# Attention weights as a product of two exponentials, with the transposed adjacency as the stationary operand

## Chip, core and metric

The kernel runs on one core of a Trainium2 chip. The metric is the device time of one execution in microseconds; the runs below are five executions of the kernel before the change. A profile is one execution recorded by the hardware profiler.

## What is computed

Four graph layers follow one another on 128 graphs of 64 nodes with 256 features. Each adds its result to its input and normalizes the rows. Layer 0 is five steps of a gated recurrent cell, layer 1 an MLP with RMS norm behind a neighbour sum, layer 2 a hyperbolic map, layer 3 an attention. The change is in layer 3:

```python
h = einsum('bnd,ed->bne', hidden, W_w) + W_b
a1, a2 = a_w[:Dh], a_w[Dh:]
e = h @ a1
f = h @ a2
logits = e[:, :, None] + f[:, None, :] + a_b[0]
u = mask * exp(logits)            # mask: the adjacency, 64 x 64 per graph
a = u / sum(u, axis=2, keepdims=True)
h_prime = einsum('bnm,bmd->bnd', a, h)
x = layernorm(x + h_prime)
```

## The kernel before

Two graphs share the 128 partitions as one block; four blocks make a group, so a group is 8 graphs, and 16 groups (NG) run through all four layers. The two graphs of a block lie on the diagonal quadrants of a 128 x 128 adjacency tile `edge` (`ed` in the code), zero elsewhere. `adjT` is its transpose, made once per group on TensorE (L620) and copied out of PSUM by VectorE (L623); L626 then turns `ed` into 0 and 1 for layer 0.

The functions `pe`, `turn`, `dve`, `act` and `pool` do not issue anything: they record an operation with its engine and an estimated cost in `Flow`. Every group is a stream of such operations, and the set-up is a stream of its own. `Flow.issue` then plans all streams together: `Plan.advance` picks, for an assumed clock of each engine, the operation that can start soonest, `ways` ranks operations by how much must follow them, several plans are kept side by side in stretches of 25 us, and the best one is issued. Up to four streams are open at once, and eight PSUM banks are shared among them (`bank`). So the order of instructions on each engine is that of the plan, and each engine works through its own in order. A change of any operation or cost lets the whole order be planned anew. Buffers come in slots by tag and group number modulo 3 (`unit`).

In layer 0 each of the five steps works on two halves of the group. `ps_hr` turns the state into rows, `ps_agg` sums neighbours with `ed`, `p_r`, `p_u`, `p_v`, `p_w`, `p_in` and `p_hn` are the gate products (L580), VectorE adds and ScalarE takes tanh. All matmuls are in fp32; the profile shows two records for each. Layer 1 has `ps_hid` and `ps_o` (line 300 is the helper `matmul`), layer 2 `ps_sup`. `layer_norm` takes statistics on VectorE, the power on GpSimd (L595, `rstd`), and writes half of the blocks on VectorE (L609), half on ScalarE (L605).

Layer 3, lines 890 to 927, for each group:

- L550 and L553: x3 is transposed on TensorE (`ps_T`), ScalarE copies it to `x3T`.
- For each of four blocks, `ps_a` (2 matmuls of 259 columns) gives h in 256 columns, one zero column, and the two sums e and f; VectorE adds the biases `wb_r` (L899) into `ho`. The added bias makes the zero column a column of ones.
- `ps_e` (L903): four transposes of one column of `ho`, repeated 128 times, bring the one sum to the free dimension; VectorE adds the other (L908) into `lg`, ScalarE takes the exponential (L911), VectorE multiplies by `adjT` (L915) into the quadrants of `ed`.
- `ps_att`: one matmul of 257 columns per block with `ed` as the stationary operand; column 256 is the sum of weights. VectorE takes the reciprocal (L922) and adds x3 (L923) to give y, and `layer_norm` follows.

The set-up loads weights and vectors (small vectors on GpSimd's DMA queue, L392 to L496), turns and combines the gate weights on TensorE, and works out the two extra columns of `wattT` and `wb_r` on VectorE (L525).

Of the kernel before, what the change touches and what calls it, by code (L numbers as in the profile page):

```python
# [13 lines left out]
AF = mybir.ActivationFunctionType  # L14
OP = mybir.AluOpType

P = 128
# [210 lines left out]
def kernel(  # L228
# [31 lines left out]
    nc = tc.nc  # L260
    B, N, D = x.shape
# [3 lines left out]
    NB = 4  # L265
    G = 2 * NB
    R = NB * P
    KD = D // P
# [11 lines left out]
    flow = Flow()  # L280
    quads = [slice(t * N, (t + 1) * N) for t in range(2)]


    def fixed(shape, name):
        return Buf(lambda: const.tile(shape, F32, name=name))

    def bank(name):
        return Buf(lambda: psum.tile([P, 512], F32, tag="bank", name=name), bank=True)

    def bufs(tag):  # L290
        return 2 if tag == "h" else 1

    def unit(tag, s, name, shape=(P, R), bufs=1):

        t = f"{tag}{s}"
        return Buf(lambda: work.tile(list(shape), F32, tag=t, name=name, bufs=bufs), slot=(t, bufs))


    def matmul(o, lhsT, rhs, k, nk):
        nc.tensor.matmul(o, lhsT, rhs, start=(k == 0), stop=(k == nk - 1))  # L300

    def pe(n, run, w, r):
        flow.op("PE", {512: 0.86, 256: 0.435, 257: 0.44, 128: 0.23}.get(n, 0.3), run, w, r)

    def turn(run, w, r):
        flow.op("PE", 0.11, run, w, r)

    def dve(n, run, w, r):
        flow.op("DVE", 0.16 + 0.00105 * n, run, w, r)

    def act(n, run, w, r):
        flow.op("ACT", 0.27 + 0.00077 * n, run, w, r)

    def pool(us, run, w, r=()):
        flow.op("POOL", us, run, w, r)
# [11 lines left out]
    def tiles_of(t):  # L327
        return t.rearrange("p (b n) -> p b n", n=P)

    def over(t, n):  # L330
        return t.unsqueeze(1).to_broadcast([P, n, t.shape[-1]])
# [19 lines left out]
    ident = Buf(lambda: ident_t)  # L351
# [26 lines left out]
    a12, na22, w_hn = gate_w("a12"), gate_w("na22"), gate_w("w_hn")  # L378
    a11, s1, s2, s3, s4, w_in = ([gate_w(f"{n}_{l}") for l in range(L)] for n in ("a11", "s1", "s2", "s3", "s4", "w_in"))

    wattT = fixed([P, KD, D + 3], "wattT")

    NV = 3 * KD
    NC = 2 * NV + 2 * KH
# [15 lines left out]
    for src, eng, tags in ((w_hh, "SP", ("h", "h")), (w_ih, "ACT", ("A", "B")), (att_w, "ACT", ("adjT",))):  # L400
        nf = src.shape[0] // P
        q = {"SP": nc.sync, "ACT": nc.scalar}[eng]
        for i, tag in enumerate(tags):
            n = min(4, nf - 4 * i)
# [53 lines left out]
    for l in range(L):  # L458
        ps = bank("ps_wmT")
# [9 lines left out]
        for k in range(KD):  # L469
            for i, n in ((0, 2 * D), (1, D)):  # L470
                ps = bank("ps_wmih")
# [19 lines left out]
    turned(att_w, KD, lambda i, k, ps: dve(256, lambda: nc.vector.tensor_copy(wattT[:, k, :D], ps[:, :D]),  # L491
                                           [(wattT, k)], [ps]))

    def everywhere(v, n, name, more=0):
        t = fixed([P, n + more], name)
        flow.op("POOL", 0.8, lambda: nc.gpsimd.dma_start(  # L496
            t[:, :n], bass.AP(tensor=v.tensor, offset=v.offset, ap=[[0, P], [1, n]])), [t])
        return t

    eps_c = everywhere(epsilon, 1, "eps_c")  # L500
    b2_r = everywhere(b2, D, "b2_r")
    wb_r = everywhere(att_b, D, "wb_r", 3)
    a_r = everywhere(a_w, 2 * D, "a_r")
    ab_c = everywhere(a_b, 1, "ab_c")

# [9 lines left out]
    junk_d = fixed([P, D], "junk_d")  # L515
# [1 line left out]

    pool(0.11, lambda: nc.gpsimd.memset(wattT[:, :, D:D + 1], 0.0), [(wattT, D)])  # L520
    pool(0.11, lambda: nc.gpsimd.memset(wb_r[:, D:D + 1], 1.0), [wb_r])
    for i in range(2):
        for o, k in ((wattT[:, 0, :], 0), (wattT[:, 1, :], 1), (wb_r.tile(), None)):
            src = wb_r if k is None else (wattT, k)
            dve(256, lambda o=o, i=i: nc.vector.scalar_tensor_tensor(  # L525
                junk_d.tile(), o[:, :D], 1.0, a_r[:, i * D:(i + 1) * D], OP.mult, OP.mult,
                accum_out=o[:, D + 1 + i:D + 2 + i]), [src if k is None else (wattT, (k, i))], [src, a_r])

    def group(g):
        s = g % NF  # L530

        def tiny(name, shape=(P, NB), dt=F32):
            t = f"{name}{s}"
            return Buf(lambda: small.tile(list(shape), dt, tag=t, name=f"{name}_{g}"), slot=(t, 2))

        def u(tag, name, shape=(P, R)):
            return unit(tag, s, f"{name}_{g}", shape, bufs(tag))

        def rows(tag, name):
            return u(tag, name, (P, NB, D))  # L540
# [4 lines left out]
        def feats_of(dst, src, n):  # L545

            ps = bank("ps_T")
            for j in range(2):
                for c in range(KD):
                    turn(lambda j=j, c=c: nc.tensor.transpose(  # L550
                        ps[:, c * HR + j * P:c * HR + (j + 1) * P], src[:, 2 * n + j, c * P:(c + 1) * P], ident.tile()),
                        [ps], [(src, 2 * n + j)])
            act(512, lambda: nc.scalar.copy(dst[:, :, half(n)], blocks_of(ps.tile())), [(dst, n)], [ps])  # L553

        def rows_of(src, n):

            ps = bank("ps_hr")
            for j in range(2):
                for c in range(KD):
                    turn(lambda j=j, c=c: nc.tensor.transpose(  # L560
                        ps[:, j * D + c * P:j * D + (c + 1) * P],
                        src[:, c, (2 * n + j) * P:(2 * n + j + 1) * P], ident.tile()), [ps], [(src, n)])
            return ps

        def aggregate(dst, src, b0, n):

            ps = bank("ps_agg")
            for j in range(2):
                for c in range(KD):
                    pe(128, lambda j=j, c=c: matmul(  # L570
                        ps[:, c * HR + j * P:c * HR + (j + 1) * P], src[:, b0 + j, c * P:(c + 1) * P],
                        ed[:, 2 * n + j, :], 0, 1), [ps], [(src, b0 + j), ed])
            act(512, lambda: nc.scalar.copy(dst[:, :, half(n)], blocks_of(ps.tile())), [(dst, n)], [ps])  # L573
            return ps
# [42 lines left out]
        ed = edge[s]  # L617
        ps = bank("ps_adjT")
# [3 lines left out]
        adjT = u("adjT", "adjT", (P, NB, P))  # L622
        dve(512, lambda ps=ps: nc.vector.tensor_copy(adjT.tile(), tiles_of(ps.tile())), [adjT], [ps])  # L623
        for t in range(2):
            q = quads[t]
# [123 lines left out]
        for n in range(2):  # L749
            ps = rows_of(hT, n)  # L750
            for j in range(2):
                b = 2 * n + j
# [5 lines left out]
        for t in range(2):  # L758
            q = quads[t]
# [3 lines left out]
        x1 = layer_norm(y0, "A", "n0")  # L763
# [8 lines left out]
        for i, tag in enumerate(("h", "h", "B", "A")):  # L772
            t = u(tag, f"hid{i}", (P, KD, R))
            hid += [(t, 0), (t, 1)]
        sqs = u("U", "sqs")
        for c in range(KH):
            ps = bank("ps_hid")
# [11 lines left out]
        ps = bank("ps_ss")  # L789
# [21 lines left out]
        for h in range(NB // 2):  # L811
            ps = bank("ps_o1")
            for j in range(2):
                b = 2 * h + j
# [4 lines left out]
            for j in range(2):  # L819
                b = 2 * h + j  # L820
# [36 lines left out]
        for h in range(NB // 2):  # L857
            for j in range(2):
                b = 2 * h + j
                pe(256, lambda b=b, j=j, ps=sup[h]: matmul(  # L860
                    ps[:, j * D:(j + 1) * D], adjT[:, b, :], tan[:, b, :], 0, 1), [sup[h]], [adjT, (tan, b)])
            for j in range(2):
                b = 2 * h + j
# [23 lines left out]
        x3 = layer_norm(y2, "B", "n2")  # L887


        x3T = u("agg", "x3T", (P, KD, R))  # L890
        for n in range(2):
            feats_of(x3T, x3, n)
        ho = u("h", "ho", (P, NB, D + 3))
        for b in range(NB):
            ps = bank("ps_a")
            for k in range(KD):
                pe(256, lambda ps=ps, b=b, k=k: matmul(
                    ps[:, :D + 3], x3T[:, k, b * P:(b + 1) * P], wattT[:, k, :], k, KD), [ps], [(x3T, b // 2), wattT])
            dve(256, lambda ps=ps, b=b: nc.vector.tensor_add(ho[:, b, :], ps[:, :D + 3], wb_r.tile()),  # L899
                [(ho, b)], [ps, wb_r])  # L900
        ps_e = bank("ps_e")
        for b in range(NB):
            turn(lambda b=b: nc.tensor.transpose(  # L903
                ps_e[:, b * P:(b + 1) * P], ho[:, b, D + 1:D + 2].to_broadcast([P, P]), ident.tile()), [ps_e], [(ho, b)])
        lg = u("U", "lg", (P, NB, N))
        for t in range(2):
            q = quads[t]
            dve(256, lambda q=q: nc.vector.tensor_tensor(  # L908
                lg[q], tiles_of(ps_e.tile())[q, :, q], ho[q, :, D + 2].unsqueeze(2).to_broadcast([N, NB, N]), OP.add),
                [(lg, t)], [ps_e, ho])  # L910
        act(256, lambda: nc.scalar.activation(lg.tile(), lg.tile(), AF.Exp, bias=ab_c.tile()), [lg], [lg, ab_c])  # L911

        for t in range(2):
            q = quads[t]
            dve(256, lambda q=q: nc.vector.tensor_mul(ed[q, :, q], lg[q], adjT[q, :, q]), [(ed, t)], [lg, adjT])  # L915
        y3 = rows("y", "y3")
        rd = tiny("rd")
        for b in range(NB):
            ps = bank("ps_att")
            pe(257, lambda ps=ps, b=b: matmul(ps[:, :D + 1], ed[:, b, :], ho[:, b, :D + 1], 0, 1),  # L920
               [ps], [ed, (ho, b)])
            dve(4, lambda ps=ps, b=b: nc.vector.reciprocal(rd[:, b:b + 1], ps[:, D:D + 1]), [(rd, b)], [ps])  # L922
            dve(256, lambda ps=ps, b=b: nc.vector.scalar_tensor_tensor(  # L923
                y3[:, b, :], ps[:, :D], rd[:, b:b + 1], x3[:, b, :], OP.mult, OP.add),
                [(y3, b)], [ps, (rd, b), (x3, b)])
        o = layer_norm(y3, "A", "n3")
        flow.op("SP", 0.1, lambda: nc.sync.dma_start(out_rows[g], o.tile()), (), [o])

    for g in range(NG):
        flow.stream()  # L930
        group(g)
# [33 lines left out]
```

## Time and profile before

| | |
|---|---|
| median of 5 runs | 2521.28 us (2518.35 to 2522.56) |
| the profiled execution | 2521.28 us, its span 2519.5 us |
| PE busy, DVE busy, ACT busy, POOL busy | 2445.8, 1658.2, 1191.4, 176.0 us |
| mean granted clock of TensorE | 0.991 |
| DMA | 35.12 MB, mean 14 GB/s |
| table loads on ScalarE | 33 of 1.28 us |

The span runs from the first to the last instruction. In a row of the timeline the columns are start, duration, engine, line, operation, output and inputs, shapes and count, and in brackets the idle time of the engine before it with what ended it. A group's row has count, busy time, mean duration in ns, and the idle time ahead. The chain of waits goes back from the last instruction: start, length, engine and line of each piece. A row of windows gives the stretch, its length, the busy time and instructions of PE, PEld, DVE, ACT and POOL, then the granted clock, the DMA share and GB/s.

### The profile page before, as it was taken

The numbers are of one execution on the slowest core, as the hardware profiler recorded it, in microseconds if no ns is written. First come the engines' busy times: TensorE is split into PE (matmuls) and PEld (weight loads), VectorE is DVE, ScalarE is ACT, GpSimd is POOL, SyncE is SP. The second block draws the span as 40 slices with busy tenths as digits, with TensorE's granted clock in tenths as the row PEclk, the third lists the DMA queues.
The fourth block names the chain that finished last, engine by engine and source line by source line (L and its number), as shares of the span: only waits on it lengthen the run. The fifth ranks groups of instructions, "written<-read, shape, count | busy, mean of one in ns | idle before, by whom it ended". The sixth has DMA issues, their size and how long they took to land.

```text
span 2519.5 us, 31834 instructions
## 1 busy us (share of the span) xinstructions
PE 2445.8 (97%) x11970; PEld 2045.1 (81%) x11970; DVE 1658.2 (66%) x3722; ACT 1191.4 (47%) x2499; POOL 176.0 (7%) x149
## 2 busy tenths in 40 slices
PE   8999999999999999999999999999999999999986
PEld 6887878888877887878878878778878878788764
DVE  3566666756776766767666766666666757576676
ACT  3444454444455445454454454464454444544452
POOL 4000000000000000000000000000000000000011
PEclk9999999999999999999999999999999999999987
DMA  4000000000000000000000000000000000000000
GB/s 124 1 9 1 19 9 1 20 9 1 9 20 9 20 1 28 1 28 3 17 9 1 28 1 1 17 19 1 28 20 1 20 9 1 28 1 1 18 9 17
DMA packets 39146, 35.12 MB, mean 14 GB/s; under 512 B 9892, under 2 KB 38592, under 8 KB 38992
## 3 DMA queue, kind: packets, MB, share of 16 engines
q1 hardware_dynamic: 34848, 28.05, 3.5%
q10 hardware_dynamic: 3744, 4.46, 0.6%
q8 instruction: 95, 1.56, 0.3%
q0 software_dynamic: 400, 0.57, 0.1%
q14 instruction: 59, 0.48, 0.1%
HBM read 24.69 MB, written 8.39 MB: 13 GB/s over the span
## 4 chain that ended last, share of the span: by engine, by line
PE 72%; DVE 12%; ACT 4%; POOL 2%; issue 1%; DMA 0%; POOLq 0%; ACTq 0%; DVEq 0%
PE ps_hid L300 8%; PE p_v L580 8%; PE p_r L580 8%; PE p_hn L580 8%; PE p_w L580 8%; PE p_in L580 8%; PE ps_o L300 8%; PE ps_agg L300 5%; PE p_u L580 4%; PE ps_hr L560 2%; PE ps_a L300 2%; POOL rstd L595 2%; DVE st L590 1%; PE ps_T L550 1%; PE ps_att L300 1%
## 5 line engine op out<-in xcount | busy, mean ns | idle before, releaser
L580 PE MATMUL p_hn<-hT,w_hn 128*128 128x256 f32 x1280 | 321.9, 379 | 0.0
L580 PE MATMUL p_in<-agg,w_in 128*128 128x256 f32 x1280 | 311.4, 379 | 0.0
L580 PEld LDWEIGHTS p_in<-agg,w_in 128*128 128x128 f32 x1280 | 240.9, 190 | 32.1 <-ACT junk_a L864 0.2
L580 PEld LDWEIGHTS p_hn<-hT,w_hn 128*128 128x128 f32 x1280 | 228.3, 191 | 26.3 <-issue 3.1
L300 PE MATMUL ps_o<-w2s,hid 128*128 128x256 f32 x1024 | 232.4, 381 | 3.9 <-DVE n L875 3.7
L300 PE MATMUL ps_hid<-aggm,w1s 128*128 128x512 f32 x512 | 228.8, 598 | 1.9 <-ACT aggm L573 1.9
L300 PEld LDWEIGHTS ps_o<-w2s,hid 128*128 128x128 f32 x1024 | 194.3, 191 | 31.1 <-ACT th L806 3.9
L595 POOL TENSOR_TENSOR rstd<-ve,pow 128x4 f32<-128x4 f32 (+1 forms) x64 | 76.5, 1196 | 1681.0 <-DVE ve L593 1680.9
L684 ACT ACTIVATE V<-V,half_b 128x256 f32<-128x256 f32 x160 | 73.3, 500 | 253.0 <-DVE V L680 253.0
L300 PEld LDWEIGHTS ps_hid<-aggm,w1s 128*128 128x128 f32 x512 | 96.5, 192 | 109.6 <-issue 102.5
L580 PE MATMUL p_w<-tA,s 128*128 128x256 f32 x640 | 160.7, 380 | 0.4 <-DVE tA L663 0.4
L580 PE MATMUL p_u<-tA,s 128*128 128x256 f32 x640 | 155.8, 382 | 4.8 <-DVE tA L663 3.9
L580 PE MATMUL p_v<-tB,na 128*128 128x256 f32 x640 | 156.6, 382 | 3.6 <-DVE V L680 3.4
L580 PE MATMUL p_r<-agg,a 128*128 128x256 f32 x640 | 155.3, 380 | 3.7 <-ACT agg L573 3.7
L693 DVE SCALAR_TENSOR_TENSOR R<-R,hnb 128x512 f32<-128x512 f32 x80 | 56.8, 710 | 153.0 <-ACT R L684 152.7
L580 PE MATMUL p_r<-hT,a 128*128 128x256 f32 x640 | 154.4, 380 | 2.4 <-ACT U L710 1.8
L580 PE MATMUL p_v<-tB,s 128*128 128x256 f32 x640 | 155.6, 379 | 0.0
L580 PE MATMUL p_w<-hT,s 128*128 128x256 f32 x640 | 154.7, 379 | 0.0
L649 ACT ACTIVATE hnb<-p_hn,half_b 128x256 f32<-128x256 f32 x320 | 136.0, 471 | 38.5 <-PE p_hn L580 37.9
L788 DVE TENSOR_TENSOR sqs<-sqs,sq 128x512 f32<-128x512 f32 x112 | 78.4, 700 | 103.0 <-ACT sq L785 102.9
L300 PEld LDWEIGHTS ps_agg<-edge,hr 128*128 128x128 f32 x1024 | 133.7, 192 | 12.9 <-ACT hr L643 5.7
L580 PEld LDWEIGHTS p_u<-tA,s 128*128 128x128 f32 x640 | 118.9, 190 | 27.3 <-DVE tA L663 6.7
(201 smaller groups left out, 4458.8 us busy)
## 6 DMA issues: line engine op xcount, KB each, us to landing
x<-in_x_dram SPq DMA_DIRECT2D x16, 512.0 KB, 3.8
xr<-in_x_dram SPq DMA_DIRECT2D x16, 512.0 KB, 3.5
out_dram<-x_n SPq DMA_DIRECT2D x16, 512.0 KB, 2.9
edge<-in_adj_dram SPq DMA_DIRECT2D x32, 64.0 KB, 2.4
wm<-in_L_gnn_weight_dram ACTq DMA_DIRECT2D x5, 256.0 KB, 10.0
w1s<-in_L_gnn_W_dram ACTq DMA_DIRECT2D x1, 1024.0 KB, 13.0
w2s<-in_L_gnn_W_dram ACTq DMA_DIRECT2D x1, 1024.0 KB, 9.1
aw_in_L_gnn_w_ih_dram<-in_L_gnn_w_ih_dram ACTq DMA_DIRECT2D x1, 512.0 KB, 5.5
```

The lines of the kernel that those rows point to most:

```text
L300: nc.tensor.matmul(o, lhsT, rhs, start=(k == 0), stop=(k == nk - 1))
L550: turn(lambda j=j, c=c: nc.tensor.transpose(ps[:, c * HR + j * P:c * HR + (j + 1) * P], src[:, 2 * n + j, c * P:(c + 1) * P], ident.tile() ...
L560: turn(lambda j=j, c=c: nc.tensor.transpose(ps[:, j * D + c * P:j * D + (c + 1) * P], src[:, c, (2 * n + j) * P:(2 * n + j + 1) * P], iden ...
L580: pe(256, lambda c=c, k=k: nc.tensor.matmul(ps[:, c * HR:(c + 1) * HR], w[:, k, c * P:(c + 1) * P], v(k), start=first and c == k == 0, sto ...
L590: dve(256, lambda b=b: nc.vector.bn_stats(st[:, b, :], y[:, b, :]), [(st, b)], [(y, b)])
L595: pool(1.1, lambda: nc.gpsimd.tensor_tensor(rstd[:, :m, :], ve[:, :m, :], pow2[:, :m, :], OP.pow), [rstd], [ve])
L649: act(300, lambda c=c: nc.scalar.activation(hnb[:, c, half(n)], p_hn[:, c * HR:(c + 1) * HR], AF.Identity, bias=half_b[:, 2 * KD + c:2 * K ...
L684: act(256, lambda c=c: nc.scalar.activation(o[:, c, :], src(c), AF.Tanh, bias=half_b[:, i * KD + c:i * KD + c + 1], scale=0.5), [(o, c)], ...
L693: dve(512, lambda: nc.vector.scalar_tensor_tensor(t.tile(), t.tile(), 1.0, hnb[:, :, half(n)], OP.add, OP.mult), [t], [t, (hnb, (n, 0)), ( ...
L788: dve(512, lambda sq=sq: nc.vector.tensor_add(sqs.tile(), sqs.tile(), sq.tile()), [sqs], [sqs, sq])
```

## The change

With e + f + b = (e + c) + (f + c), where c is half of all constant parts, the weight is a product of two exponentials, one per row and one per column. One of them scales the rows of h before the sum, and the other is applied behind it. The stationary operand of `ps_att` is then `adjT` alone. The bias of h comes out of the weighted mean unchanged, so it is added to x3 instead (one VectorE operation on 128 x 1024). `ps_a` has 258 columns, of which the last two become the exponentials (128 x 2, ScalarE); column 256 of `hw` is the column's exponential, and so gives the sum of weights. Three tiny operations per block replace the reciprocal; the last factor keeps the reference's ratio. In the set-up, the two dot products change their places, the bias needs only the sum of both halves of `a_r`, and the two memsets on GpSimd go. One cost in the planner's table changes for one-column matmuls (0.21 for 0.3).

```diff
-        flow.op("PE", {512: 0.86, 256: 0.435, 257: 0.44, 128: 0.23}.get(n, 0.3), run, w, r)
+        flow.op("PE", {512: 0.86, 256: 0.435, 128: 0.23, 1: 0.21}.get(n, 0.3), run, w, r)
...
-    wattT = fixed([P, KD, D + 3], "wattT")
+    wattT = fixed([P, KD, D + 2], "wattT")
...
-    pool(0.11, lambda: nc.gpsimd.memset(wattT[:, :, D:D + 1], 0.0), [(wattT, D)])
-    pool(0.11, lambda: nc.gpsimd.memset(wb_r[:, D:D + 1], 1.0), [wb_r])
+    cs, a_sum = fixed([P, 1], "cs"), fixed([P, D], "a_sum")
+
+    def dot(o, x0, x1, w, r):
+
+        dve(256, lambda: nc.vector.scalar_tensor_tensor(
+            junk_d.tile(), x0(), 1.0, x1(), OP.mult, OP.mult, accum_out=o()), [w], r)
+
     for i in range(2):
-        for o, k in ((wattT[:, 0, :], 0), (wattT[:, 1, :], 1), (wb_r.tile(), None)):
-            src = wb_r if k is None else (wattT, k)
-            dve(256, lambda o=o, i=i: nc.vector.scalar_tensor_tensor(
-                junk_d.tile(), o[:, :D], 1.0, a_r[:, i * D:(i + 1) * D], OP.mult, OP.mult,
-                accum_out=o[:, D + 1 + i:D + 2 + i]), [src if k is None else (wattT, (k, i))], [src, a_r])
+        for k in range(KD):
+            dot(lambda i=i, k=k: wattT[:, k, D + i:D + i + 1], lambda k=k: wattT[:, k, :D],
+                lambda i=i: a_r[:, (1 - i) * D:(2 - i) * D], (wattT, (k, i)), [(wattT, k), a_r])
+    dve(256, lambda: nc.vector.tensor_add(a_sum.tile(), a_r[:, :D], a_r[:, D:]), [a_sum], [a_r])
+    dot(lambda: cs.tile(), lambda: wb_r.tile(), lambda: a_sum.tile(), cs, [wb_r, a_sum])
+    dve(4, lambda: nc.vector.tensor_scalar(cs.tile(), cs.tile(), ab_c.tile(), 0.5, OP.add, OP.mult), [cs], [cs, ab_c])
...
-        ho = u("h", "ho", (P, NB, D + 3))
+        hw = u("h", "hw", (P, NB, D + 2))
         for b in range(NB):
             ps = bank("ps_a")
             for k in range(KD):
                 pe(256, lambda ps=ps, b=b, k=k: matmul(
-                    ps[:, :D + 3], x3T[:, k, b * P:(b + 1) * P], wattT[:, k, :], k, KD), [ps], [(x3T, b // 2), wattT])
-            dve(256, lambda ps=ps, b=b: nc.vector.tensor_add(ho[:, b, :], ps[:, :D + 3], wb_r.tile()),
-                [(ho, b)], [ps, wb_r])
-        ps_e = bank("ps_e")
-        for b in range(NB):
-            turn(lambda b=b: nc.tensor.transpose(
-                ps_e[:, b * P:(b + 1) * P], ho[:, b, D + 1:D + 2].to_broadcast([P, P]), ident.tile()), [ps_e], [(ho, b)])
-        lg = u("U", "lg", (P, NB, N))
-        for t in range(2):
-            q = quads[t]
-            dve(256, lambda q=q: nc.vector.tensor_tensor(
-                lg[q], tiles_of(ps_e.tile())[q, :, q], ho[q, :, D + 2].unsqueeze(2).to_broadcast([N, NB, N]), OP.add),
-                [(lg, t)], [ps_e, ho])
-        act(256, lambda: nc.scalar.activation(lg.tile(), lg.tile(), AF.Exp, bias=ab_c.tile()), [lg], [lg, ab_c])
-
-        for t in range(2):
-            q = quads[t]
-            dve(256, lambda q=q: nc.vector.tensor_mul(ed[q, :, q], lg[q], adjT[q, :, q]), [(ed, t)], [lg, adjT])
+                    ps[:, :D + 2], x3T[:, k, b * P:(b + 1) * P], wattT[:, k, :], k, KD), [ps], [(x3T, b // 2), wattT])
+            act(4, lambda ps=ps, b=b: nc.scalar.activation(
+                hw[:, b, D:], ps[:, D:D + 2], AF.Exp, bias=cs.tile()), [(hw, b)], [ps, cs])
+            act(256, lambda ps=ps, b=b: nc.scalar.activation(
+                hw[:, b, :D], ps[:, :D], AF.Identity, scale=hw[:, b, D:D + 1]), [(hw, b)], [ps, (hw, b)])
+        dve(1030, lambda: nc.vector.tensor_add(x3.tile(), x3.tile(), over(wb_r.tile(), NB)), [x3], [x3, wb_r])
         y3 = rows("y", "y3")
         rd = tiny("rd")
         for b in range(NB):
             ps = bank("ps_att")
-            pe(257, lambda ps=ps, b=b: matmul(ps[:, :D + 1], ed[:, b, :], ho[:, b, :D + 1], 0, 1),
-               [ps], [ed, (ho, b)])
-            dve(4, lambda ps=ps, b=b: nc.vector.reciprocal(rd[:, b:b + 1], ps[:, D:D + 1]), [(rd, b)], [ps])
+            pe(256, lambda ps=ps, b=b: matmul(ps[:, :D + 1], adjT[:, b, :], hw[:, b, :D + 1], 0, 1), [ps], [adjT, (hw, b)])
+            dve(4, lambda ps=ps, b=b: nc.vector.tensor_mul(rd[:, b:b + 1], ps[:, D:D + 1], hw[:, b, D + 1:]), [(rd, b)], [ps, (hw, b)])
+            dve(4, lambda b=b: nc.vector.reciprocal(rd[:, b:b + 1], rd[:, b:b + 1]), [(rd, b)], [(rd, b)])
+            dve(4, lambda b=b: nc.vector.tensor_mul(rd[:, b:b + 1], rd[:, b:b + 1], hw[:, b, D + 1:]), [(rd, b)], [(rd, b), (hw, b)])
```

## Prediction

> **What bounds the kernel now.** I read the page's busy times first, then PE's groups with shapes kept apart, PE's start times in the timeline, the waits, and last the chain for the final 100 us.
>
> ```profile
> span 2519.5 us, 31834 instructions
> PE 2445.8 (97%) x11970; PEld 2045.1 (81%) x11970; DVE 1658.2 (66%) x3722; ACT 1191.4 (47%) x2499; POOL 176.0 (7%) x149
> ```
>
> PE's share is modelled, so I went by start times. PE's records start 216 ns apart for a 256-column pass (two records per matmul, 0.432 us), 218 for 259 columns, 109 for a transpose. Each group's count times its own pitch gives 2412 us; PE starts at 10.3 and its last record starts at 2509.7, so 87 us are lost between: about 3 before 120 us, 45 spread in pieces of 0.3 to 2.3 us up to 2413, 40 after. So up to 2413 the time is PE's work plus a few per cent of stalls; behind it the last group runs alone and the chain is latency.
>
> **What is removed from PE.** The four transposes ps_e of each group.
>
> ```profile
> L903 PE MATMUL ps_e<-ident,ho 128*128 128x128 f32 x64 | 14.1, 277 | 1.4 <-DVE ho L899 1.3
> ```
>
> The mean of 277 ns is latency. The price is in the starts:
>
> ```profile
> 287.66 0.38 PE L903 MATMUL ps_e<-ident,ho 128*128 128x128 f32 x2
> 287.88 0.60 PE L580 MATMUL p_in<-agg,w_in 128*128 128x256 f32 x2
> 288.31 0.27 PE L903 MATMUL ps_e<-ident,ho 128*128 128x128 f32 x1
> 288.42 0.60 PE L580 MATMUL p_in<-agg,w_in 128*128 128x256 f32 x2
> ```
>
> Two transposes move the next matmul by 0.22, one by 0.11. Groups 0 to 13 do theirs under the PE bound: 56 x 0.109 = **-6.1 us**; the eight of groups 14 and 15 lie in the tail and count there. ps_a loses one column of 259: 256 passes x about 1 ns = **-0.2**.
>
> **What moves between VectorE and ScalarE.** Per group DVE loses four ho adds (0.34 each by start distance, row 421 ns), four 64x256 operations on lg and edge (0.42), and gains one 128x1024 add on x3 and eight tiny operations. The wide add has no row: between two 512-wide ones (2 x 0.60 by start distance, row 0.69) and the same shape on POOL (2.35); I take 1.2. Tiny ones are 0.08 to 0.2. That is about -3.0 + 2.2 = -0.8 us a group. ACT loses one 0.50 and gains four 128x2 exponentials (nearest row: 128x4 tanh, 0.205) and four scalings out of PSUM (nearest rows: hnb, 0.471, and x_n with a scale and a bias per partition, 0.594; I take the first, also out of PSUM): +2.2 us a group, 35 in all, on an engine busy 47%. Neither is the bound; both cost nothing while PE has other groups' matmuls between ps_a and ps_att. In the built instruction order of the changed kernel (it has no times) at least three 256-wide matmuls, 1.30 us, stand between the last ps_a and its ps_att; exp, scaling and hand-over take 0.205 + 0.471 + about 0.2. Without that cover it is the third rival.
>
> Exp and Tanh share a table already: 33 table loads stand in the order before and after. A load takes 1.28 us and the next activation starts 0.08 later (load at 2478.52, Ln at 2479.88). "ScalarE: Activation LUTs" (What ACT_TABLE_LOAD costs) of the Trainium skill adds a drain and calls a switch 2.66 us; with equal counts it would change nothing but the one chain through Ln in the tail, by an estimated +1.4 on both sides.
>
> **What is added at the start.** The changed set-up adds both halves of a_r on DVE (a_sum). In the built order this stands fifteenth on DVE, ahead of the adjT copy and the edge compares of the first group, and DVE works in order. In the trace:
>
> ```profile
> 9.06 0.55 POOL L496 DMA_DIRECT2D a_r<-in_L_gnn_a_w_dram  x1 [1.97 <-DMA vecs<-in_L_gnn_b_ih_dram]
> ...
> a_r<-in_L_gnn_a_w_dram POOLq DMA_DIRECT2D x1, 256.0 KB, 7.7
> ...
> 13.81 0.69 DVE L623 COPY adjT<-ps_adjT 128x512 f32<-128x512 f32 x1 [2.38 <-PE ps_adjT L620]
> 14.42 0.60 DVE L626 TENSOR_SCALAR edge<-edge 64x256 f32<-64x256 f32 x2
> ...
> 15.07 1.22 PE L300 MATMUL ps_agg<-edge,x 128*128 128x128 f32 x4 [1.30 <-DVE edge L626]
> ```
>
> a_r is issued at 9.06 and lands 7.7 later, at 16.8. Plus 0.1 to the reader and 0.42 for the add: the adjT copy starts at 17.3, not 13.81, and ps_agg, 1.26 behind it, at 18.55, not 15.07: **+3.5 us**. Queued behind a_sum are those copies, and PE's in-order queue waits at ps_agg. After 15.5 I find no PE stall over 0.15 us until 120 us, so nothing takes it back. Bounds: 0 (a_r lands by 13.4) to +5 (it lands 1.5 later).
>
> **The tail.** From 2413 group 15 is alone with leftovers of 14. Its end:
>
> ```profile
> 2504.11 0.44 DVE ho L899
> 2504.60 0.34 PE ps_e L903
> 2504.96 0.42 DVE lg L908
> 2505.39 0.44 DVE lg L908
> 2505.85 0.52 ACT lg L911
> 2506.39 0.43 DVE edge L915
> 2506.84 0.43 DVE edge L915
> 2507.31 3.07 PE ps_att L300 x8
> 2510.41 0.17 DVE rd L922
> 2510.58 0.08 DVE mv L591
> 2510.66 0.76 DVE y L923 x2
> ```
>
> All four ps_att wait for the last edge. Changed, each block goes alone: ps_a of block 3 is out at 2504.11, exp and scaling end about 2504.8, and block 0's ps_att is out about then. From there DVE is the limit: twelve tiny operations, four y, four statistics, about 4.5 us, so ve (before: 2512.72) comes at 2509.3: -3.4. Ahead of that, by the built order: the y and statistics of group 15 have one operation of group 14 less between them (-0.7); its hidden units no longer alternate with group 14's (-1.0), but the x3 add of group 14 now stands ahead of ve of the MLP norm (+1.15); Ln and tan come 0.55 earlier; then group 14's norm (off, a POOL pow of 1.0) stands ahead of the last th, which DVE reached without that wait before, and x3 is ready 0.65 later than before, 1.2 of it lost since tan. Sum: -0.7 + 0.65 - 3.4 = **-3.4**, bounds -7 and +1.
>
> One thing more: before ps_agg at 2427.36 PE idles 3.7 us, and the clock is 0.53 in the next 11:
>
> ```profile
> 2426.00:2437.00 11.00, 8.97 (x23) 5.81 (x24) 7.95 (x34) 6.11 (x10) 4.78 (x3) 0.53 0.00 0
> ```
>
> PE loses about 2.4 us by it. In the new order that wait is cut into about 1.9 and under 1 us. Waits of 1.4 to 1.5 at 2355 and 2359 left the clock at 1.00, so the drop may go (-2.4, within the bound of -7); I don't count on it. "TensorE: Matmul & The Clock Gate" (The HAM clock gate) of the Trainium skill halves the clock after an idle window of about 3.4 us; by that it would go, and the sum would be about 2512.7 (estimate).
>
> **The order between.** The order is planned anew as a whole, so all 45 us of stalls from 120 to 2413 are dealt again. I compared cover, PE work standing between a producer and its reader, in both orders: ps_hr to ps_agg at least 1.3 us in both; ps_agg to the first product from tA median 3.0 before, 3.3 now; the state update to the next ps_hr median 5.3 and 5.9. Nothing gets tighter; DVE, which ends most of these waits, has less to do, ACT more. I take 0, bounds -6 and +8.
>
> **Sum.** The profiled execution took 2521.28 us, also the median of the runs, 1.8 outside its span. 2521.28 - 6.1 - 0.2 + 3.5 - 3.4 = **2515.1 us**.
>
> **Rivals.**
> *The new start wait is covered or a_r comes early:* PE could have work elsewhere; against it, the PE order has ps_agg in the same place. Then 2515.1 - 3.5 = 2511.6. Or the newly dealt stalls shrink by some 4: 2511. Together 0.24.
> *The change does on PE what it says and the schedule gives it back:* stalls 3 us more, or a tail that gains only 1: 2518, no measurable difference. For it: 45 us of stalls were dealt at random, and the start already takes half of the PE gain. 0.20.
> *Slower: ps_att waits behind other groups' activations on ACT.* Where a pair of gate activations (0.91 in the timeline) stands ahead of every block, ACT needs 4 x (0.68 + 0.91) = 6.4 us against 3.5 of ps_a and 1.3 of cover: 1.6 a group, 25 in all, 2540; from about 0.7 a group, 11 in all, it turns the sign measurably. Half of that price, 2528, is the likelier size. Against it: in twelve of sixteen groups the new ACT order has two or fewer foreign instructions among the eight, in three more it has three. 0.08.
> *The forecast as it stands,* 2511 to 2519: 0.48.
>
> **Chances.** What a measurement of this kernel tells from no change is about 0.2%, 5 us: below 2516.2 is faster, above 2526.3 slower. Of the forecast's 0.48 I put 0.32 below 2516.2 and 0.16 above; with the first rival 0.24 that is 0.56 faster; 0.16 + 0.20 = 0.36 within; 0.08 slower. The range of 2508 to 2524 takes in the tail's and the order's bounds in part and leaves out about 0.1 on either side.
>
> **What the new profile would show.** Right: ps_agg's first start near 18.5 behind DVE a_sum; no ps_e; PE's groups lighter by 7 us; ps_att starting within 1 us of the last ps_a at the end, and ve 5.2 us behind the last ps_a result instead of 8.6; table loads still 33. Wrong: ps_agg still near 15; ps_att in PE's waits for ACT hw with several us; PE's stalls from 120 to 2413 away from 45 by over 6; x3's add at 2 us or more beside POOL.

## The result, and the profile after

| | |
|---|---|
| before, all runs of the comparison | 2519.78 us median (2516.09 to 2523.78, 48 runs) |
| after | 2523.98 us median (2521.77 to 2528.35, 28 runs) |
| ratio of after to before | 1.0018, 95% interval 1.0012 to 1.0023 |
| profiled execution of after | 2526.73 us, its span 2524.9 us (before: 2521.28 and 2519.5) |

The changed kernel is slower by 0.18%: inside the 0.2% that the prediction called no change, but with an interval that leaves out 1, on the other side of the forecast, and 8.9 us above it: +4.2 where -6.2 was forecast. What follows counts with the two profiled executions, which differ by 5.4 us; that of after lies 2.7 us above its median, that of before 1.5, so 1.2 of the 5.4 come from the choice of executions.

Two lines of the page of after, the span and the busy times:

```profile
span 2524.9 us, 31907 instructions
PE 2436.5 (96%) x11906; PEld 2041.3 (81%) x11906; DVE 1643.1 (65%) x3738; ACT 1228.4 (49%) x2611; POOL 177.7 (7%) x147
```

PE has 64 records fewer and is busy 9 us less, DVE is busy 15 us less, ACT 37 more, and yet the span is longer. So PE waits more. By start times (each group's count times its own median pitch, as in the prediction) PE's work fell from about 2412 to 2403 us, 7.0 of it the 64 transposes, and what it lost from 120 us to the last `p_in` (below: the stalls) rose from 45.4 to 63.0 us.

**The start.** From the DMA view and the timeline of after (start, duration, engine, line, operation, tiles):

```profile
a_r<-in_L_gnn_a_w_dram POOLq DMA_DIRECT2D x1, 256.0 KB, 7.6
```

```profile
16.97 0.42 DVE L531 TENSOR_TENSOR a_sum<-a_r 128x256 f32<-128x256 f32 x1 [5.11 <-DMA a_r<-in_L_gnn_a_w_dram]
17.31 0.68 DVE L629 COPY adjT<-ps_adjT 128x512 f32<-128x512 f32 x1
...
18.56 1.22 PE L300 MATMUL ps_agg<-edge,x 128*128 128x128 f32 x4 [4.38 <-DVE edge L632]
```

DVE sat 5.11 us in front of `a_sum`, and the first `ps_agg` came at 18.56 (forecast 18.55, before 15.07). Part of that was given back: before, 19 of the 24 `ps_w` transposes behind it started 0.17 us and more apart (most 0.213), and after only 12 of them, the others 0.11. The first product of the weights (`ps_wmih`) comes at 24.72 for 22.12, 2.6 later, and the first `p_hn` at 35.48 for 32.88, also 2.6.

**The sums over the adjacency.** PE's group of `ps_att` in after; before, it had 2.4 us of idle time ahead of it, behind `edge`:

```profile
L300 PE MATMUL ps_att<-hw,adjT 128*128 128x257 f32 x128 | 34.3, 392 | 0.0
```

**The tail.** The timeline of after at the end:

```profile
2513.09 1.90 PE L300 MATMUL ps_att<-hw,adjT 128*128 128x257 f32 x8
2513.29 0.26 ACT L907 ACTIVATE hw<-ps_a,cs 128x2 f32<-128x2 f32 x1
2513.58 0.47 ACT L909 ACTIVATE hw<-ps_a,hw 128x256 f32<-128x256 f32 x1
...
2518.18 0.16 DVE L599 TENSOR_TENSOR ve<-mv,eps 128x4 f32<-128x4 f32 x1
```

`ps_att` starts before the last block is even out, and `ve` follows the last `ps_a` (out just ahead of 2513.29) by 4.9 us, where it took 8.6 before. From the `ps_agg` at which the prediction's tail began (2427.36 before, 2439.26 after) to the end it is 85.7 us for 92.1. The windows of the 11 us from just ahead of it (busy times of five engines, then the granted clock):

```profile
2438.00:2449.00 11.00, 10.26 (x39) 5.79 (x38) 7.94 (x37) 6.72 (x12) 4.60 (x3) 1.00 0.00 1
```

The clock is 1.00 where it was 0.53: the wait of 3.7 us has become one of 1.98 at 2434.24 and one of 0.2 (all three by start times).

**The order between.** The waits view of PE from 120 us to the last `p_in`, each line with the total, the times and the longest; first before, then after:

```profile
PE p_u L580 <- DVE tA L663: 3.9, 7, 1.0
PE p_r L580 <- ACT agg L573: 3.7, 4, 1.1
PE ps_hr L560 <- DVE hT L705: 3.7, 4, 2.1
```

```profile
PE ps_hr L566 <- DVE hT L711: 7.3, 10, 1.9
PE p_r L586 <- ACT agg L579: 6.5, 6, 1.4
PE ps_T L556 <- DVE x_n L615: 4.8, 3, 3.1
...
PE p_w L586 <- DVE tA L669: 3.8, 2, 3.3
```

The new waits are for `hT`, `agg`, `tA` and `x_n`, which belong to the recurrent cell, the norms and the sums over edges. No line names `hw` or `ps_att`: the changed attention itself makes PE wait nowhere in that stretch. Stalls longer than 1 us were 14 with 18.3 us in all, and are 21 with 33.3 us: 15.0 of the 17.6 us that the stalls rose by. That is where the time went.

The longest, in the timeline of after:

```profile
769.10 2.34 POOL L776 TENSOR_TENSOR xb<-x_n,b_r 128x1024 f32<-128x1024 f32 x1 [1.66 <-DVE fac L854]
769.27 3.12 DVE L859 TENSOR_SCALAR tan<-x_n,fac 128x256 f32<-128x256 f32 x4
772.31 0.68 DVE L669 TENSOR_TENSOR tA<-ps_agg,agg 128x512 f32<-128x512 f32 x1
...
773.04 2.50 PE L586 MATMUL p_w<-tA,s 128*128 128x256 f32 x5 [3.32 <-DVE tA L669]
```

`tA` stands on DVE behind four `tan` of another group, and these run beside a wide GpSimd add: together 3.12 us, where one of them takes 0.35. The next product in PE's order needs this `tA`, and PE waits 3.32. Then it pays again, as the windows of after show:

```profile
773.00:778.00 5.00, 4.96 (x15) 4.15 (x16) 3.88 (x6) 2.23 (x5) 0.00 (x0) 0.66 0.00 0
```

For the next 5 us the clock is 0.66. In windows of 10 us between 120 and 2413 us the kernel before never shows a clock below 0.97; after has three (0.83 at 770, 0.83 at 870, 0.86 at 1370), 4.8 us of clock in all, contained in the 63.0.

**The account.** Up to the tail's first `ps_agg`, after is 11.9 us late (2439.26 less 2427.36). Of that 2.6 is the start; the 56 transposes and the columns saved 6.3; so the order cost 11.9 - 2.6 + 6.3 = 15.6. The tail took 6.4 back: 2.6 - 6.3 + 15.6 - 6.4 = 5.5, against 5.4 seen.

### The profile page after: what moved, and what is told of

Read it like the earlier page. It is cut to its first block, busy times and chain, and to the rows that moved or that the text cites. A ratio compares the mean times of both kernels' runs of the same rounds, so it can differ in the third digit from the quotient of the medians.

```text
span 2524.9 us, 31907 instructions
## 1 busy us (share of the span) xinstructions
PE 2436.5 (96%) x11906; PEld 2041.3 (81%) x11906; DVE 1643.1 (65%) x3738; ACT 1228.4 (49%) x2611; POOL 177.7 (7%) x147
## 4 chain that ended last, share of the span: by engine, by line
PE 71%; DVE 12%; ACT 4%; POOL 2%; DMA 2%; issue 1%; POOLq 0%; ACTq 0%; DVEq 0%; SPq 0%
PE ps_hid L300 9%; PE ps_o L300 9%; PE p_v L586 8%; PE p_w L586 8%; PE p_in L586 7%; PE p_r L586 7%; PE p_hn L586 7%; PE p_u L586 4%; PE ps_agg L300 4%; PE ps_a L300 2%; POOL rstd L601 2%; PE ps_hr L566 2%; DVE st L596 2%; DMA xr<-in_x_dram 2%; DVE tA L669 1%
## 6 DMA issues: line engine op xcount, KB each, us to landing
w1s<-in_L_gnn_W_dram ACTq DMA_DIRECT2D x1, 1024.0 KB, 11.9
```

## The experiments

The theory: the changed attention is worth what its parts say, and the planner, given other operations and one other cost, happened to deal an order with more stalls. Its rivals: the new instructions themselves make the stalls (ScalarE work in the way of others, the wide x3 add on DVE), or GpSimd's wide add, which now meets DVE more often, does. Every kernel was compared with before on the same chip (before's median there: 2520.16 us for the first four runs, 2518.29 for the two cost rows and the stretch of 24, 2519.08 for the rest); stalls are those of PE from 120 us to the last `p_in`, in the profiled execution.

### The start by itself

The order is that of after; only `cs` is formed otherwise, from two dot products, so that nothing waits for `a_r` ahead of the adjT copy.

```diff
-    dve(256, lambda: nc.vector.tensor_add(a_sum.tile(), a_r[:, :D], a_r[:, D:]), [a_sum], [a_r])
-    dot(lambda: cs.tile(), lambda: wb_r.tile(), lambda: a_sum.tile(), cs, [wb_r, a_sum])
+    def constant():
+        for i in range(2):
+            nc.vector.scalar_tensor_tensor(junk_d.tile(), wb_r.tile(), 1.0, a_r[:, i * D:(i + 1) * D], OP.mult, OP.mult,
+                                           accum_out=a_sum[:, i:i + 1])
+        nc.vector.tensor_add(cs.tile(), a_sum[:, :1], a_sum[:, 1:2])
+    dve(256, lambda: None, [a_sum], [a_r])
+    dve(256, constant, [cs], [wb_r, a_sum])
```

> The changed kernel in its own order, only that the sum of both halves of a_r is not formed: the constant comes from two dot products of wb_r, which stand at 46 us behind the wattT dots. Theory: the 3.5 us at the start are paid in full, so 2524.0 - 3.5 = 2520.5, and ps_agg starts near 15.1. Rival: PE takes the wait back later, then 2523 to 2524.

Measured: 2520.58 us (2518.47 to 2523.58), ratio 1.0003 (0.9995 to 1.0012); 3.4 us below after. `ps_agg` starts at 15.42 and the first `p_hn` at 33.10, 2.4 earlier than in after; stalls 59.4, 22 of them over 1 us with 34.1 in all, mostly the places of after. The profiled execution is the fastest of its 11. The start costs about what was forecast for it, and without it the kernel is still no faster than before.

### The new attention in the old order

The planner is given before's operations and costs, so that it issues before's order; only what each operation runs is changed. Places whose instruction is gone issue nothing, and the new ones take the place of the old. The core of the edit, against before:

```diff
-                    ps[:, :D + 3], x3T[:, k, b * P:(b + 1) * P], wattT[:, k, :], k, KD), [ps], [(x3T, b // 2), wattT])
-            dve(256, lambda ps=ps, b=b: nc.vector.tensor_add(ho[:, b, :], ps[:, :D + 3], wb_r.tile()),
-                [(ho, b)], [ps, wb_r])
+                    ps[:, :D + 2], x3T[:, k, b * P:(b + 1) * P], wattT[:, k, :D + 2], k, KD), [ps], [(x3T, b // 2), wattT])
+            def scaled(ps=ps, b=b):
+                nc.scalar.activation(ho[:, b, D:D + 2], ps[:, D:D + 2], AF.Exp, bias=cs.tile())
+                nc.scalar.activation(ho[:, b, :D], ps[:, :D], AF.Identity, scale=ho[:, b, D:D + 1])
+            dve(256, scaled, [(ho, b)], [ps, wb_r])
...
-            turn(lambda b=b: nc.tensor.transpose(
-                ps_e[:, b * P:(b + 1) * P], ho[:, b, D + 1:D + 2].to_broadcast([P, P]), ident.tile()), [ps_e], [(ho, b)])
+            turn(lambda: None, [ps_e], [(ho, b)])
```

> The new attention, issued in the order that was planned for the kernel before (its recorded operations and costs are kept, only what each one issues is changed; the constant from two dots, so no wait at the start). Theory that the newly dealt order made about 15 us of PE stalls: 2519.8 - 6.3 for the transposes - 3 to 6 for the tail, 2507 to 2511, with stalls from 120 to 2413 us near 45. Rival, the attention itself (exponentials and scalings on ScalarE, the wide add on VectorE) stands in the way of the other groups: 2518 or more, stalls of 55 or more.

Measured: 2507.01 us (2503.72 to 2507.91), ratio 0.9944 (0.9931 to 0.9958). Stalls 43.2. PE's waits in that stretch, the same view as above:

```profile
PE p_u L589 <- DVE tA L672: 3.9, 7, 1.0
PE p_r L589 <- ACT agg L582: 3.7, 4, 1.1
PE ps_hr L569 <- DVE hT L714: 3.0, 4, 1.4
```

The first two are before's to the tenth, the third is 0.7 lower. The stalls over 1 us are 14 with 18.4 us, before's 14 with 18.3. So the new instructions add no stalls in this order, and with it the change is worth 13 us, without the wait for `a_sum`, which this kernel leaves out. In the profile the span is 13.4 shorter: 1.0 at the start (`ps_wmih` at 21.12 for 22.12), 6.3 of PE's work, 3.3 by other stalls ahead of the last `ps_agg` (2416.73, where 2427.36 - 1.0 - 6.3 would be 2420.1), and 2.7 in the tail (89.4 for 92.1). The 6.3 and the 2.7 are terms of the forecast; whether the other 4.3 belong to the attention is not shown.

This kernel and the one of the experiment before it hold the same attention without the wait at the start and differ in their order: 2507.01 against 2520.58 us, stalls 43.2 against 59.4. So the order that was dealt anew costs 13.6 us.

### GpSimd's wide add in four parts, in after and in before

```diff
-        pool(2.35, lambda: nc.gpsimd.tensor_tensor(xb.tile(), x1.tile(), over(b2_r.tile(), NB), OP.add), [xb], [x1, b2_r])
+        def four_parts():
+            for b in range(NB):
+                nc.gpsimd.tensor_tensor(xb[:, b, :], x1[:, b, :], b2_r.tile(), OP.add)
+        pool(2.35, four_parts, [xb], [x1, b2_r])
```

> The changed kernel in its own order, with GpSimd's add of b2 (128x1024, 2.35 us, 16 times) issued as four adds of 128x256. Theory that a VectorE operation that runs beside the wide add is held up to 2 us and PE with it (nine such, 14 us of VectorE): the held time per operation falls below 0.7, and the stalls behind them (3.5 at 773, 1.6 at 1435, 1.2 at 2204, 1.2 at 1913, 1.1 at 2374) go: 2524.0 - 6 = 2518. Rival, they are only moved: 2523 to 2524.

> The kernel before in its own order, with the same split. Theory of the held VectorE: five such, 7 us; 2519.8 - 3 = 2517. Rival: 2519 to 2520.

Measured: after with the split 2519.55 us (2516.25 to 2519.88), ratio 0.9996 (0.9987 to 1.0005), 4.4 below after. Before with the split 2520.95 (2516.09 to 2522.78), ratio 1.0001 (0.9992 to 1.001). A hold is counted here where a DVE instruction beside this add lasts over 0.15 us longer than the median of its kind, with what is above the median. Counted so, after had 9 holds, 15.0 us in all (14.0 in the expectations) and 2.15 at most; with the split 13 holds, 5.1 us in all and 0.53 at most. Before had 5 holds with 7.3 us, split 8 with 3.2.

Of the five stalls that were named beforehand four are gone with the split, and the stalls over 1 us fall from 21 to 17; only the one at 773 stays, at 3.3 us. So the wide add does hold DVE, and in after's order some 4 us of the lost time are its doing; in before's order no cost of the holds is to be seen (the interval leaves room for 2 us), and in neither do they explain most of 15.6. At 769 us, where four `tan` each meet a piece, the split changes little, as its timeline shows:

```profile
767.33 2.91 POOL L779 TENSOR_TENSOR xb<-x_n,b_r 128x256 f32<-128x256 f32 x4 [1.66 <-DVE fac L858]
767.50 2.90 DVE L863 TENSOR_SCALAR tan<-x_n,fac 128x256 f32<-128x256 f32 x4
...
771.05 1.99 PE L586 MATMUL p_w<-tA,s 128*128 128x256 f32 x8 [3.11 <-DVE tA L669]
```

The wait is 3.11 us for 3.32, and this time the clock stayed at 1.00 behind it.

### The same instructions, dealt again

Two of these edits exchange one row of the planner's cost table between the kernels, four change its stretch from 25 us to 24 or 26. None changes an instruction of the program, only the order of the work (the new attention at a stretch of 26 shows 31 table loads, every other run 33).

```diff
-        flow.op("PE", {512: 0.86, 256: 0.435, 257: 0.44, 128: 0.23}.get(n, 0.3), run, w, r)
+        flow.op("PE", {512: 0.86, 256: 0.435, 257: 0.44, 128: 0.23, 1: 0.21}.get(n, 0.3), run, w, r)
```

```diff
-        flow.op("PE", {512: 0.86, 256: 0.435, 128: 0.23, 1: 0.21}.get(n, 0.3), run, w, r)
+        flow.op("PE", {512: 0.86, 256: 0.435, 257: 0.44, 128: 0.23}.get(n, 0.3), run, w, r)
```

```diff
-    WINDOW, STRETCH, WIDTH, LAG = 4, 25.0, 8, 40.0
+    WINDOW, STRETCH, WIDTH, LAG = 4, 24.0, 8, 40.0
```

Before with the new row, and after with the old:

> The kernel before with nothing changed but one row of the planner's cost table: a one-column product is planned at 0.21 us instead of 0.3 us. Every instruction is the same; only their order is dealt again. Theory of chance (each deal scatters the TensorE stalls between 120 us and the last input product by several us, whatever the attention is): the stalls may lie anywhere from 36 to 63 us where the kernel before had 45.4, and the time from 2510 to 2538 us. Theory of the attention (the new instructions themselves make the worse order): the stalls stay within 40 to 50 us and the time within 2516 to 2525 us.

> The changed kernel with the planner's cost row of before (the one-column product at 0.3 us again): same instructions as the changed kernel, another deal. Theory of chance: stalls between 120 us and the last input product anywhere from 36 to 63 us, and time from 2497 to 2526 us; above all it should often lie below the 63 us of the changed kernel. Theory of the attention: 57 to 69 us again, time 2519 to 2530 us.

With a stretch of 24:

> The kernel before with the planner's stretch of 24 us instead of 25: same instructions, another deal. Theory of chance: stalls from 36 to 63 us, time from 2510 to 2538 us. Theory of the attention: stalls 40 to 50 us, time 2516 to 2525 us.

> The changed kernel with the planner's stretch of 24 us instead of 25. Theory of chance: stalls from 36 to 63 us, time from 2497 to 2526 us, and against the kernel before at the same stretch on average 9 us less (6.3 us of TensorE work and 6.4 us of tail less, 3.5 us of start more), with a scatter as wide as that. Theory of the attention: 57 to 69 us of stalls again, time 2519 to 2530 us.

With a stretch of 26:

> The kernel before with the planner's stretch of 26 us instead of 25: same instructions, a third new deal. Theory of chance, by the deals of before measured so far (2511.9, 2519.8, 2537.4 us; stalls 44.7, 45.4, 59.4 us): 2508 to 2540 us. Theory that the old attention keeps to about 45 us of stalls and 24 was an odd one out: 2516 to 2525 us.

> The changed kernel with the planner's stretch of 26 us instead of 25. Theory of chance, by its deals so far (2504.0, 2510.5, 2524.0 us; stalls 34.1, 46.9, 63.0 us): 2498 to 2528 us, less than the kernel before at the same stretch by 9 us on average but by anything from +12 to -27 us in one pair. Theory that 25 and the new cost row hit the usual order and the two others were lucky: 2519 to 2530 us.

Measured (median in us, ratio to before with its interval, stalls in us, tail from the last group's `ps_agg`):

| planner | old attention | new attention |
|---|---|---|
| stretch 25, one-column product at 0.3 | 2519.78 (before); 45.4; 92.1 | 2503.95; 0.9943 (0.9929 to 0.9958); 34.1; 92.7 |
| stretch 25, one-column product at 0.21 | 2511.88; 0.9976 (0.9965 to 0.9986); 44.7; 87.6 | 2523.98 (after); 63.0; 85.7 |
| stretch 24 | 2537.36; 1.0076 (1.0061 to 1.0091); 59.4; 110.7 | 2510.48; 0.9968 (0.9958 to 0.9978); 46.9; 100.7 |
| stretch 26 | 2519.46; 1.0002 (0.9993 to 1.0011); 50.2; 88.1 | 2505.59; 0.9944 (0.9929 to 0.996); 45.0; 102.7 |

The deal alone moves the old attention over 25 us and the new one over 20, by edits that have nothing to do with attention. After is the slowest of the four orders of its own instructions. Put one row of its cost table back, which changes no instruction, and it is 20 us faster; the waits of PE from 120 us to the last `p_in` are then:

```profile
PE ps_hr L566 <- DVE hT L711: 3.9, 5, 2.2
PE p_r L586 <- ACT U L716: 3.2, 2, 1.7
PE p_r L586 <- ACT agg L579: 2.8, 3, 1.1
```

`hT` and `agg` are at 3.9 and 2.8 where after has 7.3 and 6.5. The theory that the attention makes the stalls falls with the three other deals of the new attention: 34.1, 46.9 and 45.0 us of stalls, where it wanted 57 to 69. The deals of the old attention tell less: with the new cost row the time (2511.88) left the attention theory's range, but the stalls (44.7) did not, and most of that gain, 4.5 us, is the tail; the stretch of 26 fits both theories. Chance as stated was itself too narrow once: 34.1 lies under its 36.

Nor does the tail go with the attention: 92.7, 85.7, 100.7 and 102.7 us with the new one against 92.1, 87.6, 110.7 and 88.1 with the old. Line by line in the table the new attention is faster by 15.8, slower by 12.1, faster by 26.9 and by 13.9; the mean, 11.1 faster, has a standard error of 8, so four pairs alone would not have told its worth. The run in the old order did, for that one order. The holds of DVE don't decide between deals either: they are 13.6 us in the new attention at stretch 26 (2505.59 us), 15.8 at stretch 24 (2510.48), and 15.0 in after.

### The best deal without the start's wait, and with the add in four parts

Both are the changed kernel with the old cost row (2503.95 us); the edits are those shown above.

> The changed kernel with the planner's cost row of before (the deal that took 2504.0 us) and without the wait at the start: cs is summed from two scalar products of wb_r with the halves of a_r instead of one with their sum, so the adjT copy no longer stands behind a_sum; the deal is otherwise the same. If the start is worth the same 3.4 us in any deal: 2500.5 us (2499 to 2502). Rival, a deal with few stalls takes the wait back by itself: 2503 to 2505 us.

> The same as the kernel without the start's wait in the deal of 2504.0 us, and GpSimd's 128x1024 add of b2 issued as four of 128x256. In that deal VectorE was held by the wide add 7 times for 9.2 us in all (the changed kernel: 9 times, 14.0 us, and the split gave 4.4 us there; the kernel before: 5 times, 7.3 us, and it gave nothing). If what VectorE is held costs TensorE its share: 2 to 4 us less than without the split, about 2497.5 us. Rival, the holds lie beside other work as in the kernel before: no difference, 2500.5 us.

Measured: without the wait 2501.93 us (2501.17 to 2503.39), ratio 0.9931 (0.9918 to 0.9943); with the split as well 2495.9 (2495.38 to 2498.09), ratio 0.9908 (0.9895 to 0.9922). The first was to tell 2500.5 from 2504 and doesn't: its interval overlaps that of the kernel with the wait. In its profile `ps_agg` is 3.2 earlier (15.24 for 18.40) but the first `p_hn` only 0.6 (35.09 for 35.67), because this time weights on ScalarE's queue landed later, PE waited 2.44 us for `hT`, and the clock was 0.68 in the 4 us behind. With the split, the first `p_hn` is at 32.53. So of the 5.8 us between the two spans 2.6 belong to the start and not to the split, and about 3.2 to the split, as expected for its theory (2 to 4). Holds fell from 10.7 to 2.4 us (8 to 6), stalls from 34.0 to 31.1. This is the fastest version of the study, 0.92% below before:

```profile
span 2494.2 us, 31963 instructions
```

## Why the prediction was right or wrong

The prediction said 2515.1 us and faster; it was 2523.98 and slightly slower.

- **PE's removed work, -6.3:** right. 64 transposes at 0.109 us are gone, and the old order with the new attention shows the term undisturbed.
- **VectorE and ScalarE at no cost under cover:** right. No PE wait names `hw`. The x3 add took 1.22 us (taken: 1.2), the scaling 0.474 (0.471), the 128x2 exponential 0.261 (0.205).
- **The start, +3.5:** the mechanism and the 18.55 were right to a hundredth; "nothing takes it back" was not. It rested on a search for stalls over 0.15 us, and transposes that start 0.213 apart and not 0.109 lose only 0.10 each: 0.9 came back by the faster `ps_w` transposes, leaving 2.6 in the profile. Taking the wait out gave 3.4 in the medians.
- **The tail, -3.4:** it gave 6.4, inside the bounds. The sum has a slip: the 0.55 by which Ln and tan come earlier is made of the -0.7, -1.0 and +1.15, and the +0.65 of x3 is counted from there, so -0.7 stands in it twice; without that it is -2.75. Of what came beyond the forecast the prediction had named a part: with the wait cut, the clock stayed at 1.00 (its 2.4 us were not measured by themselves). In the old order the wait remained at 2.46 us, the clock fell to 0.69 in the 11 us around, and the tail gave 2.7. With tails from 85.7 to 102.7 us in four deals of the new attention, what the 6.4 has beyond those 2.7 can't be told from the luck of the deal.
- **"The order between", taken as 0 with bounds -6 and +8:** this step failed. It was +15.6, nearly all of it in pieces over 1 us; the stalls of 63.0 for 45.4 are also the sign of being wrong that the prediction had named (away from 45 by over 6). The step compared medians of cover over all groups, and said that nothing gets tighter. Medians don't hold the few places where one producer comes late: seven more stalls over 1 us, among thousands of products, make 15 us, and at three places the clock went down as well. The true size of what a new deal may do was in no view of before, but the bounds were still too narrow by the prediction's own words: all 45 us were dealt again, and a sum of some 40 separate chances was given 8 us of room. The eight orders gave stalls from 34 to 63. Why this deal came out worse than others is not shown beyond single places like that at 773.
- **The rivals:** ps_att behind other groups' activations on ACT is refuted. "The schedule gives it back" is what happened, named with 3 us where it was 15.6. The range, 2508 to 2524, just held the time.

Two rules of the Trainium skill bear on what the runs showed. A `tan`, an `hT`, a `tA` or a `tB` was held up to 2.15 us beside a GpSimd add of 2.4, and up to 0.53 beside adds of a quarter; the `tA` and `tB` that were held read two tiles of SBUF, and none of those that read `ps_agg` was: "SBUF — State Buffer" (Who interferes with whom) says that VectorE with two SBUF inputs or in a two-port mode and a GpSimd instruction that reads SBUF exclude each other, the later one waiting for the whole instruction of the other. The trace agrees, and the split bears out that the instruction's length is the price.

The clock fell behind PE waits of 3.32 and 3.12 us (after, at 773 and 871; 0.50 in the 2 us from 774 and from 872), and not behind 3.11 in the run with the split, nor behind 1.82 in the tail of after. In the order of after without the start's wait the same two waits came again, 3.32 and 3.12 us: behind the first the clock fell (0.66 in the 5 us from 770), behind the second, at 868, it stayed at 1.00. "TensorE: Matmul & The Clock Gate" (The HAM clock gate) has it fall after an idle window of about 3.4 us, and says that the window runs freely, so that the point varies. The variation agrees; the length does not: it also fell behind 2.44 and 2.46 us (0.68 from 20 to 24 us; 0.69 from 2415.4 to 2426.4), and in after behind two waits of 0.90 and 0.46 us that lie 1.4 us apart (0.78 from 1376 to 1378, then 0.50; without the start's wait the same two waits left it at 1.00). Here the measurement stands.

## What to carry to other kernels

Where a planner orders the whole program, any edit of operations or costs deals every stall again: here that alone was worth 20 to 25 us, more than the change itself (13, in the one order in which it was held). So first measure a change with the order held (the new instructions issued from the places of the old), and only then search orders, by parameters that change no instruction; a forecast for a re-dealt order needs a range as wide as such deals scatter.

## What the runs showed of the hardware that was not expected

A single PE wait can be paid twice: 3.32 us of waiting for `tA` at 773 us, and then 5 us at a clock of 0.66, another 1.7. The wait for the same product, 3.11 us with the split, was followed by a clock of 1.00. The wait ahead of `a_sum` was forecast; that a part of it comes back in faster `ps_w` transposes was not: they start 0.213 us apart at first and 0.109 later, while the granted clock shows 1.00 throughout (from 15 to 22 us before, from 18.5 to 22 after).
